# A four-layer graph stack on one core: six blocks of the third layer turned by VectorE and DMAs, and a Newton step of the second layer on GpSimd

## The chip, the core and the metric

The kernel runs on one core of one Trainium2 chip. The metric is the device time of one execution in microseconds (us); lower is better. The time before is a median of 3 runs. The profile is of one more execution, which has its own time and a span from the first to the last instruction. PE is TensorE, DVE VectorE, ACT ScalarE, POOL GpSimd; SP only issues DMAs.

## The reference

Four attention layers over N = 4096 nodes with D = 256 features in float32. Each one adds its result to the features and normalises each row (`_layernorm`). The third layer, which most of the change concerns, is this (`x` the features, `adj` a 0/1 matrix of int32):

```python
h = x @ W
e = (h @ a[:D, 0])[:, None] + (h @ a[D:, 0])[None, :]
e = jnp.where(e > 0, e, 0.01 * e)
attention = softmax(jnp.where(adj > 0, e, -1e12), axis=1)
x = _layernorm(x + elu(attention @ h))
```

The second layer is attention with four heads, `softmax(q @ k.T / 8 + mask) @ v`, and a layernorm. The first is like the third with four heads, and the fourth weighs by cosine similarity.

## The kernel before

All features stay in on-chip memory as `X` (128 partitions, 32 tiles of 128 nodes, 257 columns). A layer goes over NB = 8 blocks b of QW = 512 output nodes, and in each block over the tiles j of source nodes, which are added up. Each layer has its own pools of buffers, which take the place of the pools of the layer before; a buffer waits until the tile that lay there has been used for the last time.

**Third layer** (`additive_one`). A step (b, j) of 32 x 8 has a part in `weights(b, j)`: SP loads the mask (one DMA of 512 KB for two tiles j, four buffers ahead), ScalarE makes `e` from `row` and `dst` (L432), VectorE multiplies by the mask (`prob`, L434). `sums(b, j)`, one step later, is PE's: four products of `prob` with `V[:, j, :]` into four accumulators (L440).

What a step of block 0 needs of tile j, `V`, `src` and `dst`, is itself made in block 0, two blocks of four tiles ahead. `turn(b)` is `transposed_block`: eight PE transposes of `X` into two PSUM banks (L118), which VectorE and ScalarE copy to `xT` (L120). `project(b, xT)` multiplies `xT` by the weights (L177). `fill_row(b)` spreads `src` as a row over all partitions; from block 2 on by two DMAs from GpSimd (`far`, L417, with elements of 4 bytes, then `row`, L418). For blocks 0 and 1 all this comes before the first step. `turn(n)` then comes at j = 4 (n - 2), and `project(n)` and `fill_row(n)` two steps later.

What is left of the second layer's last block runs beside the first steps: two additions of partial sums on GpSimd (`join_sums`, L664), the row sums on PE, and the last layernorm.

**Second layer** (`multi_head_attention`). For each b there are 64 steps. PE makes scores `p` (L622), ScalarE takes the exponential in place (L624), VectorE multiplies by the mask to `prob` (L634). The row sums `den` are kept up by GpSimd: for even j an addition (L641), for odd j a DMA that adds (L647). PE multiplies `prob` by `V` three steps later (L655). `finish` does the layernorm of the block before in small pieces at given steps: `begin_root` at j = 29, `end_root` at 33, which is one Newton step for an inverse root, of four VectorE operations on 128 x 4 elements (L137 to L140), and `scale_row` (L155) from 35 on.

**Order.** In the third layer PE's order is that of the program; in the second layer PE's, VectorE's and ScalarE's. The order of all other instructions on an engine's queue, GpSimd's too, is set by a planner when the program is built. Each queue runs in order, and an instruction that waits, or a DMA that waits to be issued, holds up what stands behind it. The places that set the third layer's order are these:

```python
xTs = {0: turn(0), 1: turn(1)}
project(0, xTs[0])
...
        weights(b, j)
        if b == 0 and j // QB + 2 < NB:
            n = j // QB + 2
            if j % QB == 0:
                xTs[n] = turn(n)
            elif j % QB == 2:
                project(n, xTs[n])
                fill_row(n)
```

Of the kernel before, what the change touches and what calls it, by code (L numbers as in the profile page):

```python
# [18 lines left out]
P = 128  # L19
# [9 lines left out]
def kernel(  # L29
# [81 lines left out]

    def transposed_block(sb, bank, b, copies=(nc.vector.tensor_copy, nc.scalar.copy)):

        xT = sb.tile([P, KC, QW], FP, name="xT")
        pts = [bank() for _ in range(KC)]
        for c, pt in enumerate(pts):
            for k in range(QB):
                nc.tensor.transpose(pt[:, k * P:(k + 1) * P], X[:, b * QB + k, c * P:(c + 1) * P], ident)  # L118
        for c, pt in enumerate(pts):
            copies[c](xT[:, c, :], pt)  # L120
        return xT

    def one_row(mv, k, y):
        st = fin.tile([P, 6], FP, name="bn")
# [6 lines left out]
        nc.scalar.activation(r, r, AF.Exp, scale=-0.5)  # L131
        return r

    def end_root(v, r, n):

        s = fin.tile([P, n], FP, name=f"s{n}")
        nc.vector.tensor_tensor(s, r, r, OP.mult)  # L137
        nc.vector.tensor_tensor(s, s, v, OP.mult)
        nc.vector.tensor_scalar(s, s, -0.5, 1.5, OP.mult, OP.add)  # L139
        nc.vector.tensor_tensor(r, r, s, OP.mult)  # L140

    def inverse_root(v, n):

# [26 lines left out]
    def additive_values(xT, b, groups, w_sb, V, src, dst, H, slope):  # L170

        g = 1.0 - slope
        heads = "p k (h d) -> p k h d"
        for k, n, pw in groups:
            for c in range(KC):
                for i in range(n):
                    nc.tensor.matmul(pw[:, i, :D + 2 * H], xT[:, c, (k + i) * P:(k + i + 1) * P], w_sb[:, c, :],  # L177
                                     start=(c == 0), stop=(c == KC - 1))
            t = slice(b * QB + k, b * QB + k + n)
            s, d = pw[:, :, D:D + H], pw[:, :, D + H:D + 2 * H]  # L180
            nc.scalar.activation(src[:, t, :], s, AF.Exp, scale=g)
            nc.scalar.activation(dst[:, t, :], d, AF.Exp, scale=g)
            nc.scalar.activation(V[:, t, D:], d, AF.Exp, scale=slope)
            nc.vector.tensor_tensor(V[:, t, :D].rearrange(heads, h=H), pw[:, :, :D].rearrange(heads, h=H),
                                    V[:, t, D:].unsqueeze(3).to_broadcast([P, n, H, D // H]), OP.mult)
# [196 lines left out]
    def additive_one(w_sb, slope, tail, op, follow):  # L382
# [3 lines left out]
        with ExitStack() as lay:  # L386
# [4 lines left out]
            row = keep.tile([P, N], FP, name="row")  # L391
            zp = pool(lay, "gb_z", 3)
            sb = pool(lay, "gb_sb", 2)
            mp = pool(lay, "gb_mask", 4)
            dr = pool(lay, "gb_dram", 2, space=bass.MemoryType.DRAM)

            ps = pool(lay, "gb_ps", 4, space=PSUM)
            pa = pool(lay, "gb_pa", 1, space=PSUM)
            edges = adjT.rearrange("(t p) i -> p t i", p=P)
            mask, acc, prob = {}, {}, {}  # L400

# [3 lines left out]
            def turn(b):  # L405
                return transposed_block(sb, bank, b)

            def project(b, xT, ks=range(QB)):
                groups = [(k, 1, bank().rearrange("p (n f) -> p n f", n=1)) for k in ks]
                additive_values(xT, b, groups, w_sb, V, src, dst, 1, slope)  # L410

            def fill_row(b):
                part = row[:, b * QW:(b + 1) * QW]
                if b > 1:

                    far = dr.tile([QB, P], FP, name="far")
                    nc.gpsimd.dma_start(far.rearrange("k p -> p k"), src[:, b * QB:(b + 1) * QB, 0])  # L417
                    nc.gpsimd.dma_start(part, far.rearrange("k p -> (k p)").unsqueeze(0).to_broadcast([P, QW]))  # L418
                    return
                pr = bank()  # L420
                for k in range(QB):
                    nc.tensor.transpose(pr[:, k * P:(k + 1) * P], src[:, b * QB + k, :].to_broadcast([P, P]), ident)
                nc.scalar.copy(part, pr)

            def weights(b, j):
                cols = slice(b * QW, (b + 1) * QW)
                m = b, j // MJ
                if j % MJ == 0:
                    mask[m] = mp.tile([P, MJ, QW], I32, name="mask")
                    nc.sync.dma_start(mask[m], edges[:, j:j + MJ, cols])  # L430
                e = sb.tile([P, QW], FP, name="e")
                nc.scalar.activation(e, row[:, cols], AF.Relu, bias=-1.0, scale=dst[:, j, :])  # L432
                prob[b, j] = zp.tile([P, QW], FP, name="prob")
                nc.vector.scalar_tensor_tensor(prob[b, j], e, 1.0, mask[m][:, j % MJ, :], OP.add, OP.mult)  # L434
# [27 lines left out]
            units = [(b, j) for b in range(NB) for j in range(NT)]  # L462
            with tc.manual_schedule(engines={mybir.EngineType.PE}):
                xTs = {0: turn(0), 1: turn(1)}
                project(0, xTs[0])
                project(1, xTs[1], [0, 1])
                fill_row(0)
                project(1, xTs[1], [2, 3])
                for i in range(len(units) + 1):
                    if i < len(units):  # L470
                        b, j = units[i]
                        weights(b, j)

                        if b == 0 and j // QB + 2 < NB:
                            n = j // QB + 2
                            if j % QB == 0:
                                xTs[n] = turn(n)
                            elif j % QB == 2:
                                project(n, xTs[n])
                                fill_row(n)  # L480
                    if i:
                        b, j = units[i - 1]
                        sums(b, j)
                        if (b, j) == (0, 1):
                            fill_row(1)
                        if b == 0 and j in (0, 3, 5):
                            tail(bank, (0, 3, 5).index(j))
                            if j == 5:
                                follow.start()
                        if b and j % 4 == 0 and j // 4 < QB:  # L490
                            outputs(b - 1, j // 4)
                        if b == NB - 1:
                            if j in (6, 10, 14):
                                follow.load_mask(0, (j - 6) // 4, prob[b, j][:, :1])


                            for step, first in enumerate((0, 2, 5)):
                                if j >= first and (j - first) % 4 == 0 and (j - first) // 4 < NB - 2:
                                    follow.prepare(even_bank, (j - first) // 4, step)
                        if j == NT - 1:  # L500
                            take_all(b)
# [7 lines left out]
    def multi_head_attention(w_sb, b_sb, tail, rows_of_den, narrow_edges):  # L509
# [12 lines left out]
        with ExitStack() as lay:  # L522
# [7 lines left out]
            with ExitStack() as pro:  # L530
# [14 lines left out]
                def keys(b):  # L545
                    for n, to, scale in (("k", kT, 1.0), ("q", qT, qscale)):
                        for o in range(KC):
                            pk = bank()
                            for c in range(KC):
                                nc.tensor.matmul(pk, w_sb[n][:, c, o * P:(o + 1) * P], xTs[b][:, c, :],  # L550
                                                 start=(c == 0), stop=(c == KC - 1))
                            part = to[:, o, b * QW:(b + 1) * QW]
                            nc.scalar.activation(part, pk, AF.Identity, bias=b_sb[n][:, o:o + 1], scale=scale)
                            nc.vector.tensor_reduce(big[n][:, b, o:o + 1], part, AX.X, OP.max,
                                                    apply_absolute_value=True)

                def values(b):


                    for k in range(0, QB, KC):  # L560
                        pv = pv2.tile([P, KC, D], FP, name="pv")
                        for s in range(KC):
                            for c in range(KC):
                                nc.tensor.matmul(pv[:, s, :], xTs[b][:, c, (k + s) * P:(k + s + 1) * P], w_sb["v"][:, c, :],  # L564
                                                 start=(c == 0), stop=(c == KC - 1))
                        j = 2 * (b * QB + k)
                        for n in range(2):
# [149 lines left out]
            def finish(b, j):  # L717
# [18 lines left out]
                    one_row(mvs[b], k, rows[k])  # L736
                elif j == 29:
                    roots[b] = begin_root(mvs[b])
                elif j == 33:
                    end_root(*roots[b])  # L740
                elif j in (35, 37, 39, 41):
                    k = (j - 35) // 2
                    scale_row(rows[k], mvs[b], roots[b][1], k)
# [41 lines left out]
    class Cosine:  # L785
# [24 lines left out]
        def prepare(self, bank, b, step):  # L810
# [4 lines left out]
            elif step == 1:  # L815
# [3 lines left out]
                for k in range(0, QB, 2):  # L819
                    pr = bank().rearrange("p (t n f) -> p t n f", t=2, f=P)  # L820
                    for t in range(2):
                        for c in range(KC):
                            nc.tensor.matmul(pr[:, t, :, :], xT[:, c, (k + t) * P:(k + t + 1) * P], w_sb[:, c, :],  # L823
                                             start=(c == 0), stop=(c == KC - 1))
                    for t in range(2):
                        for n in range(2):
# [16 lines left out]
    def cosine_attention(co, tail):  # L843
        MJ = co.MJ
        T, in_ = co.T, co.pool
        with ExitStack() as lay:
            sb = pool(lay, "co_sb", 3)

            pa = pool(lay, "co_pa", 1, space=PSUM)
            pz = pool(lay, "co_pz", 2, space=PSUM)  # L850
# [42 lines left out]
            for i in range(len(units) + LAG):  # L893
# [7 lines left out]
                if i >= LAG:  # L901
                    b, j = units[i - LAG]
                    if j == NT - 8:
                        y[b] = in_.tile([P, QB, D], FP, name="y")
                        nc.scalar.mul(y[b], X[:, b * QB:(b + 1) * QB, :D], 1.5)

                    if i < len(units):
# [93 lines left out]
```

## Time and profile before

| | before |
|---|---|
| median of 3 runs | 2920.45 us (2920.34 to 2920.62) |
| profiled execution | 2920.01 us, span 2918.1 |
| PE busy | 2901.0 us (99%) |
| VectorE, ScalarE, GpSimd busy | 1959.0, 1668.3, 927.0 us |
| DMA | 374.94 MB, mean 128 GB/s |
| second layer's steps | 816 to 1723 us |
| third layer | 1723 to 2236 us; block 0 until 1816, then 55.5 us for each block |

A row of the timeline has a start, a duration, an engine, a line, an operation and its output and inputs, with the count of merged instructions; in brackets stands how long the engine had been idle and what released it. L430 is line 430 of the kernel. A row of a stretch gives the busy time of each engine within it, PE's granted clock, the mean busy share of the 16 DMA engines, and GB/s. Merged durations overlap, since matmuls are pipelined: the pace of PE is the distance between starts. A matmul in float32 counts as two records, a transpose as one.

### The profile page before, as it was taken

Reading aid. Unit: us, or ns where it says so; the run is one execution under the profiler, and the core shown is the slowest. Engines: PE = TensorE matmul, PEld = TensorE weight load, DVE = VectorE, ACT = ScalarE, POOL = GpSimd, SP = SyncE. Lnnn points to the kernel's source line nnn. Section 1 sums busy time; section 2 is a strip of 40 time slices with the busy share of each in tenths; the row PEclk is TensorE's granted clock in tenths of the full one; section 3 lists DMA queues with packets and bytes.
Section 4 is the critical chain, followed back from the end, with each engine's and each line's share of the span. In section 5 each row is a group of like instructions: output and inputs, shape, how many; then the busy total and the mean of one; then the engine's idle time right before and its main releaser. Section 6 shows DMA issues by size and latency. Waiting matters only on the chain.

```text
span 2918.1 us, 50377 instructions
## 1 busy us (share of the span) xinstructions
PE 2901.0 (99%) x20269; PEld 1564.5 (54%) x20269; DVE 1959.0 (67%) x2545; ACT 1668.3 (57%) x2613; POOL 927.0 (32%) x647
## 2 busy tenths in 40 slices
PE   9999999999999999999999999999999999999998
PEld 5333333333643333333333358888888777777776
DVE  8899999997677877877877765555655323333333
ACT  7899999997356666666666654444454222222222
POOL 0010010100068888988889860000000000000000
PEclk9999999999999999999999999999999999999999
DMA  7566666664068888889889874444442333333331
GB/s 204 107 135 140 136 140 142 135 134 84 1 142 191 182 187 189 181 186 191 180 189 188 184 164 138 153 152 150 154 136 60 49 58 58 58 58 58 58 58 29
DMA packets 207148, 374.94 MB, mean 128 GB/s; under 512 B 15057, under 2 KB 90817, under 8 KB 206018
## 3 DMA queue, kind: packets, MB, share of 16 engines
q0 software_dynamic: 102304, 177.77, 38.5%
q1 hardware_dynamic: 104336, 193.69, 20.2%
q8 instruction: 159, 2.61, 0.3%
q14 instruction: 75, 0.61, 0.1%
q10 hardware_dynamic: 274, 0.26, 0.0%
HBM read 317.07 MB, written 21.04 MB: 116 GB/s over the span
## 4 chain that ended last, share of the span: by engine, by line
PE 97%; DVE 2%; ACT 0%; issue 0%; DMA 0%; DVEq 0%; SPq 0%
PE acc L274 23%; PE acc L875 15%; PE p L622 15%; PE acc L655 14%; PE acc L440 8%; PE g L440 8%; PE p L864 4%; PE g L864 3%; PE g L550 2%; PE g L177 1%; PE pv L564 1%; PE g L118 1%; PE acc L823 1%; PE acc L177 1%; DVE prob L634 1%; DVE s L139 1%
## 5 line engine op out<-in xcount | busy, mean ns | idle before, releaser
L634 DVE TENSOR_TENSOR prob<-p,mask 128x1024 f32<-128x1024 f32 x512 | 623.0, 1223 | 197.2 <-ACT p L624 193.4
L624 ACT ACTIVATE p<-p,shift 128x1024 f32<-128x1024 f32 x512 | 556.2, 1088 | 331.9 <-PE p L622 331.0
L274 PE MATMUL acc<-prob,V 128*32 128x512 f32 x6144 | 664.0, 592 | 1.2 <-DVE prob L264 1.2
L641 POOL TENSOR_TENSOR den<-den,prob 128x1024 f32<-128x1024 f32 x248 | 618.8, 2495 | 72.4 <-DVE prob L634 62.9
L261 ACT ACTIVATE prob<-row,dst 128x512 f32<-128x512 f32 x1020 | 633.2, 712 | 0.1
L264 DVE SCALAR_TENSOR_TENSOR prob<-prob,mask 128x2048 f32<-128x2048 f32 x256 | 582.7, 2288 | 24.1 <-ACT prob L261 20.4
L622 PE MATMUL p<-qT,kT 64*64 64x512 f32 x4096 | 532.7, 590 | 5.6 <-DVE prob L634 5.6
L655 PE MATMUL acc<-prob,V 64*64 64x512 f32 x4096 | 531.5, 589 | 0.0
L875 PE MATMUL acc<-X,prob 128*128 128x257 f32 x2048 | 485.2, 380 | 0.0
L875 PEld LDWEIGHTS acc<-X,prob 128*128 128x128 f32 x2048 | 388.5, 190 | 160.7 <-issue 113.4
L868 DVE TENSOR_TENSOR prob<-prob,mask 128x512 f32<-128x512 f32 x256 | 176.5, 691 | 418.8 <-ACT prob L867 417.6
L274 PEld LDWEIGHTS acc<-prob,V 128*32 128x32 f32 x6144 | 197.3, 110 | 453.1 <-issue 434.2
L91 POOL COPY tick<-prob 128x1 f32<-128x1 f32 x35 | 39.8, 1136 | 1017.5 <-DVE prob L264 644.3
L432 ACT ACTIVATE e<-row,dst 128x512 f32<-128x512 f32 x256 | 184.2, 722 | 235.1 <-DVE prob L434 209.0
L655 PEld LDWEIGHTS acc<-prob,V 64*64 64x64 f32 x4096 | 155.9, 133 | 285.3 <-issue 278.1
L622 PEld LDWEIGHTS p<-qT,kT 64*64 64x64 f32 x4096 | 153.7, 133 | 284.4 <-issue 255.7
L434 DVE SCALAR_TENSOR_TENSOR prob<-e,mask 128x512 f32<-128x512 f32 x256 | 178.5, 698 | 185.7 <-PE acc L440 94.5
L808 POOL DMA_DIRECT2D mask<-in_adjT x64 | 47.5, 743 | 633.8 <-DVE prob L868 509.7
L647 POOL DMA_DIRECT2D den<-prob x240 | 225.9, 941 | 28.0 <-DVE prob L634 21.0
L867 ACT ACTIVATE prob<-p 128x512 f32<-128x512 f32 x144 | 85.8, 596 | 260.1 <-PE p L864 246.0
L440 PE MATMUL g<-V,prob 128*128 128x257 f32 x1024 | 225.6, 380 | 0.0
L440 PE MATMUL acc<-V,prob 128*128 128x257 f32 x1024 | 225.1, 380 | 0.0
(154 smaller groups left out, 1972.2 us busy)
## 6 DMA issues: line engine op xcount, KB each, us to landing
mask<-in_adjT SPq DMA_DIRECT2D x256, 512.0 KB
den<-prob POOLq DMA_DIRECT2D x240, 512.0 KB, 5.3
mask<-edges SPq DMA_DIRECT2D x256, 128.0 KB
mask<-in_adjT POOLq DMA_DIRECT2D x64, 512.0 KB, 5.6
edges<-in_adj POOLq DMA_DIRECT2D x32, 512.0 KB, 9.8
den<-prob SPq DMA_DIRECT2D x16, 512.0 KB
row<-far SPq DMA_DIRECT2D x7, 1024.0 KB
X<-in_x SPq DMA_DIRECT2D x7, 512.0 KB
```

The lines of the kernel that those rows point to most:

```text
L261: nc.scalar.activation(z[:, h, :], r, AF.Relu, bias=-1.0, scale=dst[:, j, h:h + 1])
L264: nc.vector.scalar_tensor_tensor(z, z, 1.0, mask[m][:, j % MJ, :].unsqueeze(1).to_broadcast([P, H, QW]), OP.add, OP.mult)
L274: nc.tensor.matmul(acc[b][h * G:(h + 1) * G, n, :], part, prob[b, j][:, h, :], start=(j == 0), stop=(j == NT - 1))
L440: nc.tensor.matmul(acc[b][k][:, :D + 1], prob[b, j][:, k * P:(k + 1) * P], V[:, j, :], start=(j == 0), stop=(j == NT - 1))
L622: nc.tensor.matmul(p[c * d:(c + 1) * d, r, :], kT[half, c, j * d:(j + 1) * d], qT[half, c, cols], start=True, stop=True)
L624: nc.scalar.activation(p, p, AF.Exp, bias=shift)
L634: nc.vector.tensor_tensor(z, p, mask[m][:, j % MJ, :].unsqueeze(1).to_broadcast([P, KC, QW]), OP.mult)
L641: nc.gpsimd.tensor_tensor(to, to, flat, OP.add)
L647: nc.gpsimd.dma_start(to, flat, accum_op=OP.add)
L655: nc.tensor.matmul(acc[b][c][r * d:(r + 1) * d, :], V[half, j, r * d:(r + 1) * d], prob[b, j][half, r, :], start=(j == 0), stop=(j == NH - 1))
L864: nc.tensor.matmul(p, T[:, 0, j * P:(j + 1) * P], T[:, 1, cols], start=True, stop=True)
L875: nc.tensor.matmul(acc[b][k], prob[b, j][:, k * P:(k + 1) * P], X[:, j, :], start=(j == 0), stop=(j == NT - 1))
```

## The change

For blocks 2 to 7 of the third layer, PE's transposes and the two copies are replaced. VectorE transposes every 32 x 32 square of the block (`squares`, two instructions), one DMA writes the 512 KB to DRAM, and four DMAs bring them back so that each of four groups of 32 partitions holds its features. All are issued by GpSimd. The nodes of the four tiles then come in another order: tile a holds nodes a*32 to a*32 + 31 of each of the four groups of 128. So the masks of tiles 8 to 31 are loaded in that order, one DMA of 256 KB for each tile, and the `far` DMA is split in four. `turn_apart(2)` is called before the first `project`, and then `turn_apart(n + 1)` where `turn(n)` was. In the second layer `end_root` runs on GpSimd, at j = 31. In the fourth layer the tile `y` gets a pool of its own. The other lines only give `xT` its four tiles as a dimension (`xT[:, c, k]`).

```diff
+    def turned_apart(once, dr, part, to, eng):
+        B = P // QB
+        squares = once.tile([P, QB, KC, P], FP, name="squares")
+        for c in range(KC):
+            nc.vector.transpose(squares[:, :, c, :].rearrange("p q (k n) -> p k q n", n=B),
+                                part(c).rearrange("p k (q f) -> p k q f", f=B))
+        far = dr.tile([QB, B, QB, KC * P], FP, name="squares_far")
+        eng.dma_start(far.rearrange("a f q m -> (a f) (q m)"), squares.rearrange("p q c m -> p (q c m)"))
+        for q in range(QB):
+            eng.dma_start(to[q * B:(q + 1) * B], far[:, :, q, :].rearrange("a f m -> f a m"))
+        return to.rearrange("p a (c m) -> p c a m", c=KC)
+
+    def block_apart(sb, once, dr, b, eng):
+        xT = sb.tile([P, KC * QW], FP, name="xT").rearrange("p (a m) -> p a m", a=QB)
+        return turned_apart(once, dr, lambda c: X[:, b * QB:(b + 1) * QB, c * P:(c + 1) * P], xT, eng)
...
-    def end_root(v, r, n):
+    def end_root(v, r, n, eng=nc.vector):
...
+            tp = pool(lay, "gb_turn", 1)
...
+            apart = adjT.rearrange("(b k a n) i -> b a k n i", k=QB, a=QB, n=P // QB)
...
+            def turn_apart(b):
+                return block_apart(sb, tp, dr, b, nc.gpsimd)
...
-                    far = dr.tile([QB, P], FP, name="far")
-                    nc.gpsimd.dma_start(far.rearrange("k p -> p k"), src[:, b * QB:(b + 1) * QB, 0])
-                    nc.gpsimd.dma_start(part, far.rearrange("k p -> (k p)").unsqueeze(0).to_broadcast([P, QW]))
+                    far = dr.tile([QB, QB, P // QB], FP, name="far")
+                    for k in range(QB):
+                        at = slice(k * P // QB, (k + 1) * P // QB)
+                        nc.gpsimd.dma_start(far[k].rearrange("a n -> n a"), src[at, b * QB:(b + 1) * QB, 0])
+                    nc.gpsimd.dma_start(part, far.rearrange("k a n -> (k a n)").unsqueeze(0).to_broadcast([P, QW]))
...
-                    nc.sync.dma_start(mask[m], edges[:, j:j + MJ, cols])
+                    if j < 2 * QB:
+                        nc.sync.dma_start(mask[m], edges[:, j:j + MJ, cols])
+                    else:
+                        for s in range(MJ):
+                            nc.sync.dma_start(mask[m][:, s, :], apart[j // QB, j % QB + s, :, :, cols])
...
                 xTs = {0: turn(0), 1: turn(1)}
+                xTs[2] = turn_apart(2)
...
-                            if j % QB == 0:
-                                xTs[n] = turn(n)
+                            if j % QB == 0 and n + 1 < NB:
+                                xTs[n + 1] = turn_apart(n + 1)
...
-                elif j == 33:
-                    end_root(*roots[b])
+                elif j == 31:
+                    end_root(*roots[b], nc.gpsimd)
...
+            yp = pool(lay, "co_y", 2)
...
-                        y[b] = in_.tile([P, QB, D], FP, name="y")
+                        y[b] = yp.tile([P, QB, D], FP, name="y")
```

More of the change, by code (lines that the diff above doesn't have):

```diff
@@ L112, in transposed_block @@
     def transposed_block(sb, bank, b, copies=(nc.vector.tensor_copy, nc.scalar.copy)):
-        xT = sb.tile([P, KC, QW], FP, name="xT")
+        xT = sb.tile([P, KC * QW], FP, name="xT").rearrange("p (c i) -> p c i", c=KC)
         pts = [bank() for _ in range(KC)]
@@ L120, in transposed_block @@
             copies[c](xT[:, c, :], pt)
-        return xT
+        return xT.rearrange("p c (k i) -> p c k i", i=P)
+    def turned_apart(once, dr, part, to, eng):
[12 more added lines that the diff above has]
+        return turned_apart(once, dr, lambda c: X[:, b * QB:(b + 1) * QB, c * P:(c + 1) * P], xT, eng)
     def one_row(mv, k, y):
@@ L132, in first_root @@
         return r
-    def end_root(v, r, n):
+    def end_root(v, r, n, eng=nc.vector):
         s = fin.tile([P, n], FP, name=f"s{n}")
[L137 to L140, printed above, removed]
+        eng.tensor_tensor(s, r, r, OP.mult)
+        eng.tensor_tensor(s, s, v, OP.mult)
+        eng.tensor_scalar(s, s, -0.5, 1.5, OP.mult, OP.add)
+        eng.tensor_tensor(r, r, s, OP.mult)
     def inverse_root(v, n):
@@ L176, in additive_values @@
                 for i in range(n):
-                    nc.tensor.matmul(pw[:, i, :D + 2 * H], xT[:, c, (k + i) * P:(k + i + 1) * P], w_sb[:, c, :],
+                    nc.tensor.matmul(pw[:, i, :D + 2 * H], xT[:, c, k + i], w_sb[:, c, :],
                                      start=(c == 0), stop=(c == KC - 1))
@@ L549, in keys @@
                             for c in range(KC):
-                                nc.tensor.matmul(pk, w_sb[n][:, c, o * P:(o + 1) * P], xTs[b][:, c, :],
+                                nc.tensor.matmul(pk, w_sb[n][:, c, o * P:(o + 1) * P],
+                                                 xTs[b][:, c].rearrange("p k i -> p (k i)"),
                                                  start=(c == 0), stop=(c == KC - 1))
@@ L563, in values @@
                             for c in range(KC):
-                                nc.tensor.matmul(pv[:, s, :], xTs[b][:, c, (k + s) * P:(k + s + 1) * P], w_sb["v"][:, c, :],
+                                nc.tensor.matmul(pv[:, s, :], xTs[b][:, c, k + s], w_sb["v"][:, c, :],
                                                  start=(c == 0), stop=(c == KC - 1))
@@ L822, in prepare @@
                         for c in range(KC):
-                            nc.tensor.matmul(pr[:, t, :, :], xT[:, c, (k + t) * P:(k + t + 1) * P], w_sb[:, c, :],
+                            nc.tensor.matmul(pr[:, t, :, :], xT[:, c, k + t], w_sb[:, c, :],
                                              start=(c == 0), stop=(c == KC - 1))
```

## The prediction

> **What bounds the kernel now.** I read the busy times first, then the time for which TensorE (PE) waits, then the timeline of the two places that the change touches, and last the DMA share of the third layer.
>
> ```profile
> span 2918.1 us, 50377 instructions
> PE 2901.0 (99%) x20269; PEld 1564.5 (54%) x20269; DVE 1959.0 (67%) x2545; ACT 1668.3 (57%) x2613; POOL 927.0 (32%) x647
> ```
>
> From PE's table of waits (us in total, times, longest) and the timeline of the second layer:
>
> ```profile
> PE p L622 <- DVE prob L634: 5.6, 8, 0.8
> ```
>
> ```profile
> 992.44 2.62 POOL L641 TENSOR_TENSOR den<-den,prob 128x1024 f32<-128x1024 f32 x1
> 992.58 2.51 DVE L139 TENSOR_SCALAR s<-s 128x4 f32<-128x4 f32 x1
> ...
> 996.49 1.09 PE L622 MATMUL p<-qT,kT 64*64 64x512 f32 x8 [0.67 <-DVE prob L634]
> ```
>
> PE is busy 99% of the span, so time is won only by taking PE work away or closing one of its few gaps, and lost by opening a gap. Of the 17 us in which PE is idle, 5.6 are waits of the second layer's scores for `prob`, eight times. One (0.81) is at that layer's start; the other seven follow the Newton step: GpSimd starts its `den` addition at 992.44, VectorE's `tensor_scalar` of four elements starts at 992.58 and takes 2.51 us (0.17 elsewhere), and PE then stands for 0.67 us. The timeline of the third layer's first block, the stretch of a later block, and SP's row there:
>
> ```profile
> 1755.38 1.04 PE L118 MATMUL g<-ident,X 128*128 128x128 f32 x8
> 1756.26 3.63 PE L440 MATMUL acc<-V,prob 128*128 128x257 f32 x16
> ```
>
> ```profile
> 1930.00:1985.00 55.00, 55.00 (x255) 48.12 (x255) 30.86 (x69) 24.68 (x38) 0.00 (x0) 1.00 0.47 153
> ```
>
> ```profile
> L430 SPq DMA_DIRECT2D mask<-in_adjT x63: 367/368/368, 1881.6 to 2097.6; - x63
> ```
>
> In the third layer's first block the eight transposes of one `turn` hold PE for 1756.26 - 1755.38 = 0.88 us. The window row (columns: span, then PE, weight loads, VectorE, ScalarE, GpSimd, clock, DMA share, GB/s) shows a later block: PE full, the 16 DMA engines busy 0.47 of the time at 153 GB/s. Nearly all of that is masks: one 512 KB mask tile for every two steps (3.47 us). A DMA engine thus moves 153 / (0.47 x 16) = 20.3 GB/s while busy. In the densest stretches it is 343 GB/s at a share of 0.93 (1810 to 1816 us), 23.0 per engine. **This row matters most below.**
>
> [...]
>
> **The change part by part.**
> (a) Newton step to GpSimd, seven times in the middle of the second layer. VectorE loses 0.15 + 0.16 + 2.53 + 0.16 = 3.0 us each, and PE its gap: 7 x 0.67 = **4.7 us gained**. GpSimd gets four tiny operations; the nearest row is L91's copy of one column (185 ns at least, median 314), so 0.7 to 1.3 us. It has room: its additions and DMA issues leave some 100 us idle in about 900. `scale_row` four steps (6.9 us) later now waits for GpSimd; an addition in progress (2.5) plus 1.3 is 3.8 us, so that is covered. If not, VectorE stops and the gain goes: 0 to 4.7, I take 4.7.
>
> (b) 48 transposes less on PE: 6 x 0.88 = 5.3, but the first `turn` filled a wait for the first `prob` (VectorE ends it at 1732.49, PE then starts at 1732.74), so that one gives only 0.25: **4.6 us**. Twelve PSUM copies (0.68 on VectorE, 0.59 on ScalarE) go; twelve VectorE transposes of 512 elements come. The trace has none: as cheap as a 512-element copy (0.68), or twice that; VectorE is 54% busy there, so nothing on the path either way.
>
> (c) The new way of block 2: `squares`, one 512 KB DMA out, four back, all on GpSimd's queue. The masks start at 1722.90, when the second layer's V comes free, and `squares` in the same region can't be earlier. VectorE: 0.69 (`kept`) + 1.49 (`xT`) + 2 x 0.68, so 1726.4. GpSimd adds `den` until 1726.3 and issues L647 until 1727.1, then the way out. L647 landed at 1735.2 (8.8 us where 4.8 is the median), because four masks are in flight; the way out lands at 1735 to 1737. The second L664 (2.35 us) waits for L647 on the same queue. Then four issues of 0.77, and 3 to 4 us to land: 1741 to 1744. PE wants `project(2)` at 1734.3: **a wait of 7 to 10 us**, 4 at the best (nothing in the way), 16 at the worst (the way out behind the second L664). Behind it on PE stand the sums of steps 1 and later.
>
> (d) Blocks 3 to 7: per block ten issues on GpSimd (one out, four back, four `far`, one `row`): 1.0 + 3.1 + 3.1 + 0.6 = 7.8 us, and two waits in its order, for the way out (5) and for `far` (9 to 11 in the trace). One after the other that is 20 us or more against PE's 10.4 per block; interleaved, 8 to 15. So 0 to 45 us, 0 to 12 likely.
>
> (e) The masks of steps 8 to 31: two DMAs of 256 KB in place of one of 512. SP issues in 0.37 us, two in 3.47: nothing. But the source is now 4 groups of 32 rows (`b a k n i`: k with a stride of 128 rows, n with one), its slowest dimension is 4[...]. Each then carries 524,288 / 4 = 131,072 B for two steps: 6.46 us at 20.3 GB/s, 5.70 at 23.0. **PE needs the tile every 3.47 us.** The four mask buffers lead by four pairs only and drain within a block.
>
> Take 21.5 GB/s, between the two rates: 6.1 us for a new pair, 1.5 for one of the four old ones; a block of outputs takes 12 x 6.1 + 4 x 1.5 = 79.2 us[...], against 55.5 on PE. Blocks 1 to 6: 6 x 23.7 = 142. Block 7 has 86 us of PE work (the preparation of the fourth layer fills the waits): 4, a guess from 0 to 10. Block 0 has 84 of PE work against 79 of masks, 13 of what the engines did there besides (0.46 x 84 less 16 pairs), and 6 x 1.05 MB / 16 / 21.5 GB/s = 18 for the ways out and back, less 6 for pairs loaded ahead: 104, so 20. It takes in (b), (c) and (d), whose waits lie beside it. **Sum: +166.** From both ends: 23.0 GB/s gives 74.1 per block, 112 + 10 + 0 = 122; 20.3 gives 83.9, 170 + 30 + 8 = 208. Not below nothing if four engines hold the load: to keep up they would need 31 GB/s each, half again what the trace has. If the load spreads over 16, the part costs nothing, as the same bytes in the same 2 KB rows come in.
>
> The `y` pool moves without an operation: nothing.
>
> **Sum.** The profiled execution took 2920.0 us (span 2918.1 and 1.9 around it), 0.4 below the median of 2920.45. -4.7 + 166 gives **3081**; between 3035 and 3125.
>
> **The rivals.**
> 1. Masks on four engines, as above. Against it: [...]no row shows a DMA of such shape. For it: once it holds, the price follows from rows. 0.68.
> 2. The masks spread as before, and the ways out and back are late: -4.7 - 4.6 + 10 (c) + 4 (d) = +5, so 2925; 2915 to 2950. It decides as soon as `project(2)` waits over 9.3 us, which is what both parts save. For it: L647's 8.8 us. 0.18.
> 3. The other side: masks as before and the transfers land early enough, that is, the waits of (c) and (d) stay below 3.5 us: -9.3 + 2, so 2913; 2910 to 2914. It needs the way out to land in 5 us while the DMA share is 1.0. 0.12.
> 4. The Newton step on GpSimd does not do what it says (VectorE waits for it): 4.7 us more in any of these, 0.1 of the chance within each.
> The last 0.02 is for a fifth thing, such as mask loads so late that they hold up the fourth layer's first ones.
>
> **The numbers.** Within 0.2% (5.8 us, about what a measurement of this kernel can tell from no change) lies about half of case 2 and a little of case 3: 0.11. Faster: most of case 3 and a tenth of 2: 0.13. Slower: 0.76. The likeliest case's own range is 3035 to 3125; the range that holds 8 in 10 must reach down into case 2, so 2920 to 3120.
>
> **What would show it.** Right: in the third layer's blocks 1 to 6 VectorE's L434 of steps 8 to 31 waits for the DMA `mask`, PE is busy about 0.7 of those stretches, the DMA share falls towards 0.33 at about 107 GB/s, and a pair of steps takes 6 us where the first eight steps run at 1.74 each. In the second layer PE's row of waits keeps one of 0.8 us, and L139 no longer shows 2.5. In block 0, `project(2)` starts at 1741 or later. Wrong: blocks 1 to 6 at 55.5 us, the share at 0.47. Then the four-engine step has failed, and the result lies within 30 us of before.

## The result and the profile after

The changed kernel takes **3049.72 us** (median; 3048.58 to 3050.52) against 2920.34 for the kernel before in the same comparison: ratio **1.0444**, 95% interval 1.0432 to 1.0456. It is slower by 129 us, as forecast in direction and kind. The forecast of 3081 was 31 us too high. Times within a kernel are those of its profiled execution. The lines have moved: L434 of before is L465 after, L440 is L471, L177 is L196, L430 is L461, L622 is L655 and L664 is L697. The new transposes are L130, the way out to DRAM L133 and the way back L135.

The head of the profile page after:

```profile
span 3048.0 us, 50473 instructions
PE 2932.9 (96%) x20221; PEld 1557.7 (51%) x20221; DVE 1940.6 (64%) x2523; ACT 1665.2 (55%) x2607; POOL 957.1 (31%) x723
```

PE has 48 records fewer, the transposes, and yet a longer busy time: 2932.9 against 2901.0. The span has grown by 130 us, so idle time is now 115 us where it was 17. Four rows of PE's table of waits (us in total, times, longest) and one of the page's costliest groups say where it stands:

```profile
PE acc L471 <- DVE prob L465: 48.9, 54, 8.8
PE g L471 <- DVE prob L465: 35.1, 49, 2.0
PE g L196 <- DMA xT<-squares_far: 16.7, 5, 5.4
PE p L655 <- DVE prob L667: 0.8, 1, 0.8
```

```profile
L465 DVE SCALAR_TENSOR_TENSOR prob<-e,mask 128x512 f32<-128x512 f32 x256 | 175.3, 688 | 289.7 <-DMA mask<-in_adjT 240.8
```

PE waits for `prob`, and VectorE, which makes `prob`, waits 240.8 us for mask DMAs. A wait is followed through two rows here: PE's row names VectorE, but VectorE works no longer on a tile than before (688 ns against 698); the third column of its group names the transfer. In the chain that ended last, DMA now holds 12%, nearly all of it masks:

```profile
PE 82%; DMA 12%; DVE 3%; SPq 1%; issue 1%; POOL 1%; ACT 0%; DVEq 0%; POOLq 0%
```

A later block in the timeline of VectorE, and then two stretches (columns as before: span, PE, weight loads, VectorE, ScalarE, GpSimd, clock, DMA share, GB/s), the first with old and new tiles, the second with tiles in the new order alone:

```profile
2020.36 0.69 DVE L465 SCALAR_TENSOR_TENSOR prob<-e,mask 128x512 f32<-128x512 f32 x1 [1.95 <-DMA mask<-in_adjT]
2023.01 0.69 DVE L465 SCALAR_TENSOR_TENSOR prob<-e,mask 128x512 f32<-128x512 f32 x1 [1.95 <-DMA mask<-in_adjT]
```

```profile
2040.00:2110.00 70.00, 58.96 (x255) 46.78 (x254) 30.52 (x68) 24.13 (x38) 0.00 (x0) 1.00 0.35 118
2012.00:2052.00 40.00, 32.74 (x137) 24.65 (x135) 10.38 (x15) 10.82 (x15) 0.00 (x0) 1.00 0.27 100
```

One tile of 262,144 B comes every 2.64 us, which is 99.3 GB/s. The DMA share is low, 0.27, while everything waits for DMA. **The low mean share was no sign that DMA had room.** The trace also holds the start and the duration of every DMA packet: from 2018 to 2048 us, four mask packets of 2 KB are in flight for 0.82 of the time and five for 0.18. So the load moves as four streams at a time. Each carries a quarter of the rate, 24.8 GB/s, or 2,048 B in 82.6 ns; on which engine, the packets do not say. A packet is recorded with 84 ns, so neighbours in one stream overlap a little, which fits the moments with five.

### The profile page after: what moved, and what is told of

It is laid out like the page before. It is cut to its first block, busy times and chain, and to the rows that moved or that the text cites. A ratio compares the mean times of both kernels' runs of the same rounds, so it can differ in the third digit from the quotient of the medians.

```text
span 3048.0 us, 50473 instructions
## 1 busy us (share of the span) xinstructions
PE 2932.9 (96%) x20221; PEld 1557.7 (51%) x20221; DVE 1940.6 (64%) x2523; ACT 1665.2 (55%) x2607; POOL 957.1 (31%) x723
## 4 chain that ended last, share of the span: by engine, by line
PE 82%; DMA 12%; DVE 3%; SPq 1%; issue 1%; POOL 1%; ACT 0%; DVEq 0%; POOLq 0%
PE acc L293 22%; PE acc L910 14%; PE p L655 14%; PE acc L688 14%; DMA mask<-in_adjT 10%; PE p L899 4%; PE g L899 3%; PE g L471 2%; PE g L582 2%; DMA xT<-squares_far 1%; PE acc L471 1%; SPq L461 1%; PE g L196 1%; DVE prob L465 1%; PE pv L597 1%; PE acc L857 1%
## 5 line engine op out<-in xcount | busy, mean ns | idle before, releaser
L674 POOL TENSOR_TENSOR den<-den,prob 128x1024 f32<-128x1024 f32 x248 | 625.6, 2523 | 72.8 <-DVE prob L667 66.0
L655 PE MATMUL p<-qT,kT 64*64 64x512 f32 x4096 | 532.3, 590 | 0.8 <-DVE prob L667 0.8
L465 DVE SCALAR_TENSOR_TENSOR prob<-e,mask 128x512 f32<-128x512 f32 x256 | 175.3, 688 | 289.7 <-DMA mask<-in_adjT 240.8
L655 PEld LDWEIGHTS p<-qT,kT 64*64 64x64 f32 x4096 | 154.3, 133 | 277.4 <-issue 261.6
L471 PE MATMUL acc<-V,prob 128*128 128x257 f32 x1024 | 241.3, 389 | 48.9 <-DVE prob L465 48.9
L471 PE MATMUL g<-V,prob 128*128 128x257 f32 x1024 | 238.7, 385 | 35.1 <-DVE prob L465 35.1
L471 PEld LDWEIGHTS acc<-V,prob 128*128 128x128 f32 x1024 | 191.6, 192 | 96.4 <-DVE prob L465 70.9
```

Source lines behind the costliest of these rows:

```text
L471: nc.tensor.matmul(acc[b][k][:, :D + 1], prob[b, j][:, k * P:(k + 1) * P], V[:, j, :], start=(j == 0), stop=(j == NT - 1))
L655: nc.tensor.matmul(p[c * d:(c + 1) * d, r, :], kT[half, c, j * d:(j + 1) * d], qT[half, c, cols], start=True, stop=True)
L674: nc.gpsimd.tensor_tensor(to, to, flat, OP.add)
```

## The experiments

The stretches that the experiments are compared by are the third layer's blocks, each from one block's first reciprocal (at its end) to the next one's, and block 0 from the end of the second layer's steps. Before, block 0 takes 92.6 us and blocks 1 to 6 take 55.5 each; after, 133.6 and 71.7.

### The Newton step alone

```diff
-                elif j == 33:
-                    end_root(*roots[b])
+                elif j == 31:
+                    end_root(*roots[b], nc.gpsimd)
```

with `eng` in place of `nc.vector` in `end_root`. Nothing of the third layer is changed.

> The kernel before with the second layer's Newton step on GpSimd at j = 31, and nothing of the third layer. My theory: PE's seven gaps close and nothing takes their place. In the changed kernel's trace the layer's steps take 900.7 us (814.8 to 1715.5) against 907.2 before (815.7 to 1722.8), so 6.5 us less: about 2914. The prediction's own term was 4.7 (2915.6). The rival, that VectorE waits for GpSimd at scale_row or that GpSimd's additions fall behind, gives 2920 or more.

Measured: 2913.39 us, ratio 0.9977 (0.9969 to 0.9985). GpSimd's timeline and PE's wait for scores in this kernel:

```profile
987.19 0.19 POOL L137 TENSOR_TENSOR s<-r 128x4 f32<-128x4 f32 x1
987.46 0.20 POOL L138 TENSOR_TENSOR s<-s,v 128x4 f32<-128x4 f32 x1
987.75 0.19 POOL L139 TENSOR_SCALAR s<-s 128x4 f32<-128x4 f32 x1
988.02 0.20 POOL L140 TENSOR_TENSOR r<-r,s 128x4 f32<-128x4 f32 x1
988.50 0.88 POOL L647 DMA_DIRECT2D den<-prob  x1 [0.28 <-issue]
```

```profile
PE p L622 <- DVE prob L634: 0.8, 1, 0.8
```

The step takes 1.3 us of GpSimd up to its next DMA issue, and seven of the eight waits are gone. `scale_row` does not wait for it. This part is a gain of 6.6 us, so rival 4 falls. Engine and step (31 for 33) were changed together; what each gives alone was not run.

### The mask loads alone, in four, eight and two groups

Three kernels are the kernel before with nothing but the loads of tiles 8 to 31 changed: one DMA of 256 KB per tile, from rows in G groups, with G = 4 as in the change, 8 or 2. `X` and `V` stay in the old order, so these tiles get the masks of other nodes; bytes, row length (2 KB) and the number of DMAs are the same in all three.

```diff
+            apart = adjT.rearrange("(b k a n) i -> b a k n i", k=G, a=QB, n=P // G)
...
-                    nc.sync.dma_start(mask[m], edges[:, j:j + MJ, cols])
+                    if j < 2 * QB:
+                        nc.sync.dma_start(mask[m], edges[:, j:j + MJ, cols])
+                    else:
+                        for s in range(MJ):
+                            nc.sync.dma_start(mask[m][:, s, :], apart[j // QB, j % QB + s, :, :, cols])
```

**Four groups:**

> The kernel before with only the mask loads of tiles 8 to 31 taken as in the changed kernel: two DMAs of 256 KB for two tiles, source in 4 groups of 32 rows. PE still makes the transposes, so the mask rows are not those of the nodes in V. Theory (4 engines carry the load): blocks 1 to 6 go from 55.5 to about 72 us as in the changed kernel, a pair of tiles to 5.3 us; 6 x 16.6 = 100, and 5 to 25 more in block 0: 3025 to 3045. Rival (what costs is the new way of the blocks in block 0, and the masks follow from late blocks): within 5 us of 2920.

**Eight groups:**

> As the run with four groups, but the source in 8 groups of 16 rows: the same number of DMAs, bytes, rows of 2 KB and masks of other nodes. Theory (the count of the slowest dimension sets the number of engines): 8 engines at 24.8 GB/s bring a pair in 2.6 us, less than PE's 3.47, so 2920 to 2926, with a DMA share of about 0.47 in the later blocks. Rival (rows in groups, or DMAs of 256 KB, are slow in themselves, whatever the number of engines): 3020 or more as with four groups.

**Two groups:**

> As masks_four_groups, but the source in 2 groups of 64 rows (masks of other nodes again). Theory (the engines are as many as the slowest dimension counts, each at the 24.8 GB/s that the changed kernel showed): a pair of tiles takes 524,288 / 2 / 24.8 GB/s = 10.6 us, and a block 12 x 10.6 and the 8.8 that the four old pairs took in masks_four_groups (72.1 - 12 x 5.28), about 136 us. Blocks 1 to 6 give 6 x 80 = 483 more than 55.5, block 7 some 50, block 0 some 80 to 110: 3530 to 3570. Rival (a rate that is bound elsewhere, so that two engines do better or worse each): blocks under 120 or over 150 us.

| | us | ratio (95%) | a tile every | blocks 1 to 6, each |
|---|---|---|---|---|
| eight groups | 2920.19 | 1.0001 (0.9993 to 1.0010) | PE's pace | as before |
| four groups | 3045.89 | 1.0430 (1.0414 to 1.0446) | 2.64 us | 72.0 us |
| two groups | 3533.51 | 1.2099 (1.2076 to 1.2121) | 5.27 us | 133.6 us |

VectorE's timeline with four groups:

```profile
2024.52 0.69 DVE L439 SCALAR_TENSOR_TENSOR prob<-e,mask 128x512 f32<-128x512 f32 x1 [1.94 <-DMA mask<-in_adjT]
2027.17 0.69 DVE L439 SCALAR_TENSOR_TENSOR prob<-e,mask 128x512 f32<-128x512 f32 x1 [1.96 <-DMA mask<-in_adjT]
```

and with two:

```profile
2108.20 0.69 DVE L439 SCALAR_TENSOR_TENSOR prob<-e,mask 128x512 f32<-128x512 f32 x1 [4.58 <-DMA mask<-in_adjT]
2113.48 0.69 DVE L439 SCALAR_TENSOR_TENSOR prob<-e,mask 128x512 f32<-128x512 f32 x1 [4.59 <-DMA mask<-in_adjT]
```

and the stretch of a later block with eight:

```profile
1930.00:1985.00 55.00, 55.00 (x255) 48.13 (x254) 30.87 (x69) 24.57 (x38) 0.00 (x0) 1.00 0.47 152
```

Half the groups double the time of a tile: 262,144 / 5.27 / 2 = 24.9 GB/s for each of two, 24.8 for each of four. With eight, VectorE waits for a mask once in the whole layer, for 1.1 us. The packets agree: with two groups, two are in flight for 0.91 of the time from 2100 to 2150 us; with four, four for 0.85 of the time from 2022 to 2048 us; with eight, eight is the commonest number from 1930 to 1985 us; in the kernel before, from 1930 to 1985 us, it is sixteen, apart from the time with none. Their median is 84 ns in all four. So the number of streams follows the slowest dimension of the source, 2, 4 and 8 here, though the destination has 128 partitions. That four engines would carry the load was an assumption of the prediction, for which before has no row. The rows and packets show as many streams as groups, with two and with four at the same rate each (24.9 and 24.8); which engines carry them, they do not show. Where an expectation says engines, what was measured are streams. Two DMAs for one, or the strided order as such, are excluded as the cause by the eight groups, which have both.

Four groups alone cost 126 us, nearly the change's 129, and without the gain of the Newton step. In block 0 they cost 32 us (124.6 against 92.6), though PE still transposes there: the wait for a mask grows to 6 to 10 us about once per block of nodes, beside the `far` and `row` DMAs. Single mask packets are in flight for up to 7.7 us there, where 84 ns is the median. What holds them was not separated.

### The change with its masks loaded for 32 partitions at a time

The changed kernel, with each pair of tiles loaded by four DMAs of 128 KB, one for each group of 32 partitions. The slowest dimension is then 32 instead of 4; order and bytes are those of the change.

```diff
-            apart = adjT.rearrange("(b k a n) i -> b a k n i", k=QB, a=QB, n=P // QB)
+            apart = adjT.rearrange("(b k a n) i -> b k n a i", k=QB, a=QB, n=P // QB)
...
-                        for s in range(MJ):
-                            nc.sync.dma_start(mask[m][:, s, :], apart[j // QB, j % QB + s, :, :, cols])
+                        B = P // QB
+                        for k in range(QB):
+                            nc.sync.dma_start(mask[m][k * B:(k + 1) * B],
+                                              apart[j // QB, k, :, j % QB:j % QB + MJ, cols])
```

> The changed kernel, but each pair of tiles 8 to 31 loaded by four DMAs of 128 KB, one for each group of 32 rows, so that the slowest dimension on both sides is 32; the masks arrive in the same places, and the output is the reference's. Theory: [...]blocks 1 to 6 go back to 55.5 us (-100). What is then left against before is block 0 with its waits for the blocks turned by DMA (16.7 us in PE's table, and 8.8 for the first step) less 4.6 of transposes and 6.5 of the Newton step: 2925 to 2940. Rival 1 ([...]four issues for a pair are too many for SP): still over 2960. Rival 2 (block 0's waits came from the slow masks too): 2911 to 2916.

Measured: 2939.34 us, ratio 1.0067 (1.0055 to 1.0080). The stretch of a later block, and PE's waits:

```profile
1925.00:1980.00 55.00, 55.00 (x255) 48.12 (x254) 31.07 (x69) 24.49 (x38) 0.00 (x0) 1.00 0.53 151
```

```profile
PE acc L473 <- DVE prob L467: 15.6, 3, 9.8
PE g L196 <- DMA xT<-squares_far: 8.1, 3, 5.7
```

PE is full again from block 1 on (55.5 us each), so loads that fill 32 partitions at a time cost nothing here; how many streams carry them was not shown. 110 of the 129 us are gone. That is less than the 126 that the masks cost alone: in block 0 the masks alone cost 32 us, the new ways alone 26 (118.6 against 92.6), and both together 41, since PE waits for the two side by side.

What stays, +19, is block 0: +26 less the 6.6 of the Newton step. It can be added up from the pages. PE's waits are 15.6 + 8.1 = 23.7. The Newton step alone shortens the span by 7.1 us (2918.1 to 2911.0) and leaves PE busy for 2898.3; with 5.3 of transposes less, 2893.0 would be due here, and 2901.9 is measured, 8.9 more. 23.7 + 8.9 - 5.3 - 7.1 = 20.2, against 20.6 between the two spans. Of the 8.9, 5.8 stand in three groups of PE that ran slowly after the waits of 9.80 and 5.71 us (3.79, 4.65 and 6.56 us for 2.00, 3.66 and 3.66), with the clock at half after such waits (see the last section); the rest was not taken apart.

### What makes block 0 late

In the timeline after, first VectorE and then GpSimd at the third layer's start:

```profile
1731.46 0.71 DVE L130 STREAM_TRANSPOSE squares<-X 128x512 f32<-128x512 f32 x1 [8.82 <-DMA squares_far<-squares]
...
1733.02 0.65 DVE L465 SCALAR_TENSOR_TENSOR prob<-e,mask 128x512 f32<-128x512 f32 x1
```

```profile
1726.12 2.33 POOL L697 TENSOR_TENSOR den<-den 128x1024 f32<-128x1024 f32 x1 [5.85 <-DMA den<-prob]
1728.40 0.61 POOL L133 DMA_DIRECT2D squares_far<-squares  x1
1732.02 0.58 POOL L135 DMA_DIRECT2D xT<-squares_far  x1 [3.01 <-DMA squares_far<-squares]
```

The transposes at 1731.46 are those of **block 3**. There is one `squares` buffer, they wait until block 2's way out has read it, and the planner had put them ahead of the first `prob` in VectorE's order. GpSimd issues that way out only behind the second L697. So the first `prob` is 8.8 us late, and PE with it. The next kernel is that of the section above (masks for 32 partitions at a time) with VectorE's transposes kept behind the newest `prob`:

```diff
             def turn_apart(b):
-                return block_apart(sb, tp, dr, b, nc.gpsimd)
+                with tc.issue_after(newest[0]) if newest else nullcontext():
+                    return block_apart(sb, tp, dr, b, nc.gpsimd)
...
-                nc.vector.scalar_tensor_tensor(prob[b, j], e, 1.0, mask[m][:, j % MJ, :], OP.add, OP.mult)
+                ins = nc.vector.scalar_tensor_tensor(prob[b, j], e, 1.0, mask[m][:, j % MJ, :], OP.add, OP.mult)
+                newest[0] = getattr(ins, "ins", ins)
```

> As after_masks_on_16, and VectorE's transposes of the third and later turned blocks are kept behind the newest prob instruction in its order, so that the first prob no longer stands behind a transposition that waits for the only squares buffer (9.8 us in PE's table of after_masks_on_16). Theory (GpSimd's chain for block 2 is the next thing late): its xT lands at about 1740 as before, PE now waits at project(2) in place of the first sums, and the time stays: 2934 to 2941. Rival (the hold-up of VectorE was the price itself): 9 to 10 us less, 2928 to 2931.

Measured: 2943.46 us, ratio 1.0077 (1.0064 to 1.0089). No gain, and 2.5 us above the range expected. PE's timeline and waits in this kernel:

```profile
1740.10 5.24 PE L196 MATMUL g<-w_sb,xT 128*128 128x258 f32 x16 [12.16 <-DMA xT<-squares_far]
```

```profile
PE g L196 <- DMA xT<-squares_far: 26.4, 4, 12.2
```

The wait has moved to `project(2)`, whose features come by GpSimd's chain of addition, way out and way back. Taking the queue position away showed what was late next. So block 2 is given back to PE, there are two `squares` buffers, and each later block is asked for one block earlier:

```diff
-            tp = pool(lay, "gb_turn", 1)
+            tp = pool(lay, "gb_turn", 2)
...
-                xTs[2] = turn_apart(2)
...
+                xTs[2] = turn(2)
+                xTs[3] = turn_apart(3)
...
-                            if j % QB == 0 and n + 1 < NB:
-                                xTs[n + 1] = turn_apart(n + 1)
+                            if j % QB == 0 and n + 2 < NB:
+                                xTs[n + 2] = turn_apart(n + 2)
```

(the masks of tiles 8 to 11 and block 2's `far` are again those of before)

> As squares_after_prob, but block 2 is turned by PE as before (its masks in the old order) and blocks 3 to 7 by VectorE and DMAs, each asked for one block earlier, with two squares buffers. Theory (block 0 pays because the first DMA block comes too late, the later ones because GpSimd's queue takes over 10 us per block): the wait of block 2 goes, so 9 to 12 us less than 2939; of the other waits (15.6 - 9.8 and 8.1) 0 to 12 remain: 2912 to 2926. With no wait left it would be 2913.4 (newton_only) less 5 x 0.88: 2909. Rival (the waits come from the queue alone and move to block 3): 2934 or more.

Measured: 2926.74 us, ratio 1.0021 (1.0014 to 1.0027), 0.7 us above the range expected; the table of waits has 10.3 us for `xT`, three times. A further kernel on top of it also asks for `far` and `row` of blocks 2 to 7, which no step of block 0 needs, at steps 26 to 31 of the program. The aim was to take them out of GpSimd's queue between the ways:

```diff
-                                fill_row(n)
+                        if b == 0 and j >= NT - NB + 2:
+                            fill_row(j - NT + NB)
```

> As block2_on_pe, with the far and row DMAs of blocks 2 to 7 asked for at steps 26 to 31 of block 0, at the end of the program's order for that block; their rows are needed from block 2 of the outputs on. Theory (waits of row for far on GpSimd's queue hold up the ways back): 2909 to 2914, and no wait over 1 us of PE for xT. Rival (the ways out and back take that long by themselves): the same as block2_on_pe within 2 us.

Measured: 2919.55 us, ratio 0.9996 (0.9988 to 1.0004). 7 us better, but not below 2914 as expected, and PE still waits for `xT` for 8.1 us, up to 4.8 at once. GpSimd's timeline in this kernel:

```profile
1738.90 0.55 POOL L133 DMA_DIRECT2D squares_far<-squares  x1
1750.21 2.19 POOL L135 DMA_DIRECT2D xT<-squares_far  x4 [10.76 <-DMA squares_far<-squares]
```

The edit did not do what it was for: the planner sets GpSimd's order, and in the trace 15 issues of L449 and L450 (`far` and `row` of blocks 3 to 7) start between 1757 and 1799 us, as many as in the kernel before this one, only in another order among the ways back. So neither theory nor rival was tested, and where the 7 us come from is not shown. What the rows do show is a landing: between them GpSimd stands for 10.76 us until a way out has landed, and the ways back stand behind it.

### Only four blocks turned

Blocks 4 to 7 alone, the ways out and back asked for separately with a block between them, the rest as in the last kernel. The difference to that kernel, without the bodies of `out_apart` and `back_apart` and the lines that give block 3 the order of before:

```diff
-                xTs[3] = turn_apart(3)
+                out_apart(4)
...
-                            if j % QB == 0 and n + 2 < NB:
-                                xTs[n + 2] = turn_apart(n + 2)
+                            if j == 0:
+                                out_apart(5)
+                            elif j == 4:
+                                xTs[3] = turn(3)
+                            elif j in (8, 12):
+                                out_apart(n + 2)
+                            if j in (4, 8, 12, 16):
+                                xTs[n + 1] = back_apart(n + 1)
```

> Only blocks 4 to 7 are turned by VectorE and DMAs; the way out and the way back of a block are asked for separately, out for block 4 before the first step, two squares buffers, [...]rows late, VectorE's transposes behind the newest prob, Newton step on GpSimd. If every xT is there in time: newton_only's 2913.4 less 4 x 0.88, 2909 to 2911, faster than both kernels and than newton_only. If the ways out and back still come late by a few us at one or two blocks, as in block2_on_pe_rows_late (8.1 in all, with five blocks): 2913 to 2918, and the transposes on PE were the cheaper way.

Measured: 2915.13 us, ratio 0.9985 (0.9978 to 0.9991), with this wait left on PE:

```profile
PE g L196 <- DMA xT<-squares_far: 4.3, 2, 2.5
```

32 transposes save 32 x 0.11 = 3.5 us, and the waits of 4.3 take them back. The Newton step alone has the lowest time here, 2913.39, though its interval overlaps that of the four blocks; both **beat the kernels before and after**. No form of turning blocks by VectorE and DMAs that ran here gained anything over the Newton step alone: it removes at most 5.3 us of PE work. Ways out and back that SP issues, or a way out ahead of the second L697 on GpSimd, were not tried.

## Why the prediction was right, and where its sizes were off

- **The total.** 3050 against 3081 is nearer than its parts. Blocks 1 to 6 were put 45 us too high, block 7 5 too high, block 0 21 too low, and the Newton step's gain 2 too low. That these errors partly cancel is luck; that masks in four groups decide is not.
- **What bounds the kernel; PE full.** Held: with the masks loaded for 32 partitions at a time, the difference adds up from PE's waits, its work and its slower clock.
- **(a) Newton step, -4.7.** Right that the gaps close; why L139 takes 2.51 us beside GpSimd's addition and 0.17 elsewhere was not shown. 6.5 to 6.6 measured, in the change (second layer's steps 900.7 us against 907.2) as alone. The term took the idle time of 0.67 from the row. The distance between starts there is 996.49 - 994.78 = 1.71 us where 0.86 is the pace: a gap costs 0.85, or 6.0 for seven, since in a full pipeline a row's modelled end (1.04 us after its start) overlaps the next start, and across a gap it doesn't.
- **(b) VectorE's transposes.** 0.70 us measured (690 to 712 ns), 0.68 taken.
- **(c) Block 2's way.** The way out did fall behind the second L697, the "16 at the worst" order, but it then landed in 3.0 us. `project(2)` started at 1737.31, which looks earlier than the "1741 or later" of the forecast; but the third layer starts at 1715.5 us after and at 1722.8 before. Counted from there it is 21.8 us, where 1741 is 18.2, so this sign came true. Wrong about where the wait stands: the prediction put it on `project(2)`; with one `squares` buffer and the planner's order it stood on the first `prob` (8.8 us). It says "nothing on the path either way" of VectorE's transposes; that step failed, since it priced their duration and not their wait. With them pinned, the wait on `project(2)` was 12.2.
- **(d) GpSimd's queue, 0 to 12.** An issue takes 0.55 us (1.65 for three), less than the 0.77 to 1.0 taken. The waits between issues were what counted: with the masks loaded for 32 partitions at a time the sum of (b), (c) and (d) was +26 in block 0, where -4.6 + 10 + 4 = +9 was taken. The slower clock after waits, in no term, is about 6 of the difference.
- **(e) Masks on four engines.** Four at a time is right, and shown as streams by two, four and eight groups; that the streams are engines remains an assumption. Mis-sized is the rate: 21.5 GB/s was taken between two rates that the mean share gives (20.3 and 23.0); a stream carries 24.8. A pair of steps takes 2 x 2.64 = 5.28 us, not 6.1. By the prediction's own working a block is then 12 x 5.28 + 4 x 1.3 = 68.6 us; measured 71.7, and the last 3.1 are not explained. For blocks 1 to 6 it makes +97, where +142 was taken. Block 7: -0.8 for +4. Block 0: +41 for +20; four groups alone already cost +32 there, so the masks' own share was put too low, and the waits of (c) add the rest. Together -6.5 + 97 - 0.8 + 41 = +131.
- **What would show it.** The wait of L465 for `mask`, the row of 0.8 us and the DMA share (0.35 at 118 GB/s for 0.33 at 107) came as named. PE's busy share in the slow stretch is 0.82 for "about 0.7": a step that waits has its eight records counted as 2.00 us in 2.64 (0.76), of which some 0.27 is the modelled end of the last matmul, and the stretch begins with steps that waited little.
- **Rival 2**, masks spread and ways late, is the run with masks for 32 partitions at a time: 2939 where 2925 was put (range 2915 to 2950). Rival 3 never came about: even two `squares` buffers and earlier ways left 4 to 10 us of waits.

## What to carry to other kernels

When a load is given a new order of rows, look at the slowest dimension of its access pattern before the bytes: here 4 instead of 128 took the load from hidden, with a DMA share of 0.47, to a wait of 241 us, and splitting it by that dimension into four DMAs gave it back. A transfer that replaces PE work must be priced with its whole chain (the buffer that it is read from, the queue that issues it, the landing) against the microseconds that it removes; 0.88 us of PE per block stood against a chain of 9 (way out issued at 1728.40, `project(2)` at 1737.31). Look in the trace whether an edit of the program's order arrived in the queue: where a planner sets the order, it need not. Move parts one at a time: the small part that was won here (6.6 us) was hidden under the large one that was lost.

## What the runs showed of the hardware

**The clock after waits.** PE's granted clock is 1.00 in a full block but fell to 0.50 after long waits of PE. Two stretches of block 0 after, the second within the first, and then one matmul group in PE's timeline there, which took 3.65 us in the kernel before:

```profile
1783.00:1793.00 10.00, 7.48 (x27) 6.27 (x28) 2.20 (x5) 1.19 (x12) 1.92 (x4) 0.83 0.43 140
1786.50:1789.80 3.30, 3.30 (x9) 2.65 (x8) 0.85 (x2) 0.60 (x6) 0.56 (x1) 0.50 0.28 81
```

```profile
1785.52 5.41 PE L196 MATMUL g<-w_sb,xT 128*128 128x258 f32 x16 [4.18 <-DMA xT<-squares_far]
```

So a mean between 0.50 and 1.00 is a stretch with both clocks in it: the clock records of this trace have no other value, and those at half in block 0 last 3.41, 6.83 or 10.24 us. With two groups VectorE waits 4.6 us for every tile. PE's own waits are shorter, and long and short ones alternate, with a fast and a slow step:

```profile
2108.94 3.54 PE L445 MATMUL acc<-V,prob 128*128 128x257 f32 x8 [3.27 <-DVE prob L439]
2114.23 2.00 PE L445 MATMUL acc<-V,prob 128*128 128x257 f32 x8 [1.74 <-DVE prob L439]
```

A whole block ran so:

```profile
2300.00:2436.00 136.00, 85.63 (x259) 61.96 (x260) 32.76 (x72) 25.41 (x39) 0.00 (x0) 0.76 0.18 63
```

In the later blocks after, where PE's gaps are 0.65 us, the clock stays at 1.00 (the stretches of the first section). In block 0 of the changed kernel, of the run with four groups and of the five runs with masks for 32 partitions at a time, all thirteen waits of PE of 3.7 us or more were followed by half clock; of the ten between 1.8 and 3.6 us four were (1.93, 2.07, 3.06 and 3.27) and six were not; of the shorter ones none was. What decides in between was not shown. So a long wait cost more than its length, here 5.41 - 3.65 = 1.8 us on top of 4.18.

**The rate of one stream.** 24.8 to 24.9 GB/s on 2 KB rows for each group's stream, the same with two and with four groups; bytes by mean busy share had given 20.3 to 23.0, so the share did not measure what a stream carries.
